# A mixture-of-experts stage whose short last groups become single tiles of their own

## The chip, the cores and the metric

The kernel runs on one core of a Trainium2 chip. The metric is the device time of one execution in microseconds, taken as the median of several executions. The engines are named as in the profile: PE is TensorE (PEld its weight loads), DVE is VectorE, ACT is ScalarE, POOL is GpSimd, SP is SyncE.

## The reference

The reference is a small network layer over 4 x 1024 tokens of 256 channels in fp32: a recurrent block, then an attention block, then a mixture of four experts, with normalizations and residual sums around them. The change touches the mixture alone. What it computes, cut to that part:

```python
logits = xf @ gate_w.T                      # xf: (4096, 256), E = 4 experts, K = 2
probs = softmax(logits)
topv, topi = top_k(probs, K)
topv = topv / (topv.sum(-1, keepdims=True) + 1e-08)
wts = zeros((N, E)).at[arange(N)[:, None], topi].add(topv)
o0 = gelu(xf @ e0_up.T) @ e0_down.T                                   # HID = 512
o1 = silu(xf @ e1_w1.T) * (xf @ e1_w2.T) @ e1_down.T
o2 = gelu(gelu(gelu(xf @ e2_l1.T) @ e2_l2.T) @ e2_l3.T) @ e2_l4.T
o3 = gelu(gelu(xf @ e3_down.T) @ e3_up.T) @ e3_out.T
moe = sum over e of wts[:, e:e+1] * o_e       # first 64 channels set to zero
x = x + layernorm(x_in_block + moe)
```

Every token uses exactly two of the four experts, so there are six kinds of tokens, one for each pair of experts.

## The kernel before

Nearly all of the program is written as streams of operations (generators that yield an `Op` with engine, cost, priority and the events that it needs). `Plan.run` interleaves the streams by the earliest start that its cost model gives, and the order that comes out is the fixed order of the instructions on each engine. An engine runs its instructions strictly in that order, so an instruction that waits holds up all that stand behind it on its engine.

The expert stage works on kinds. `experts_input` gives every token a place in the list of its kind with matrix products, and writes the lists to `ids` (for each of 6 kinds 32 columns of 128 token numbers; unused places point at a row of zeros). The counts of the six kinds go to `counts`, and each engine loads them into registers once (L1614).

A kind is worked on in groups of N = 256 tokens, that is two tiles of 128 (`NT2 = 2`). For each group:

- `fetch` gathers the rows of the tokens from DRAM with one indirect DMA for each tile (L1414, on POOL, tiles `rwfirst`, `rwsecond`, `rwnext`);
- `turn` scales the rows on DVE (L1428), transposes them on PE (L1435) into a PSUM bank, and copies them to SBUF on ACT (L1441);
- `group` multiplies with the weights of the two experts: `products` on PE (L1456 for the hidden layers, 256 tokens wide; L1475 for the down products, one for each tile), `activations` on ACT (L1516 gelu, L1523 tanh) with two DVE products for the gated expert 1 (L1526, L1532), `outputs` on DVE (L1543), and `last`, which normalizes (DVE L1556, L1557, L1568, L1571; POOL L1562, L1563) and scatters the rows to the output (L1574, on POOL).

The kinds follow each other in the order 3, 0, 1, 2, 4, 5. The first group of each kind is always run; each further group stands inside an `If` on the count of the kind (L1620), nested in the group before. Where the `If` is not taken, every engine jumps behind all the further groups of the kind. At the place that it jumps to it brings its semaphores to the values that they would have had; POOL does so with `INC_SWDGE_SEM` for those of its DMAs. On PE a hint for the branch is given a group ahead (L1595).

What is prepared in a group for later ones stands in the list `then`: the rows of the second next group of the kind are fetched, the next group is turned, and in the first group of a kind the rows of the first two groups of the second next kind are fetched and the first group of the next kind is turned. The first group of kind 3 (`EARLY`) is run while the gates of the last tokens are still being computed, and has a list of its own.

PSUM banks are split by whether a group is a kind's first (`"first"`: two banks for hidden layers, one for outputs) or a later one (`"next"`: three and one), with one bank for all transposes (`tbanks`).

## Time and profile before

| | |
|---|---|
| median of 3 executions | 1489.87 us |
| lowest and highest | 1489.75 and 1490.87 us |
| time of the profiled execution | 1487.5 us |
| its span, first to last instruction | 1485.7 us |
| mean granted PE clock | 0.943 |
| PE, DVE, ACT, POOL busy | 1327.7, 873.2, 723.9, 467.5 us |
| last instruction of PE that is busy ends | about 1464 us |

The span is counted from the first instruction. In the lists in order of time the columns are start, duration, engine, line, operation, the tiles written and read, and in brackets the idle time of the engine ahead of the instruction and what ended it. In the list of stages the columns are the stretch, its length, the busy time of PE, PEld, DVE, ACT and POOL with the number of instructions, the granted PE clock, the busy share of the DMA engines and the rate in GB/s. A name with a `q` behind the engine (`POOLq`) is that of the engine's sequencer; its branches, semaphore instructions and drains are not counted as busy. For a line of the kernel the profile gives the durations in ns as least, median and greatest, and the times of the first and last.

### The profile page before, as it was taken

Reading aid. Unit: us, or ns where it says so; the run is one execution under the profiler, and the core shown is the slowest. Engines: PE = TensorE matmul, PEld = TensorE weight load, DVE = VectorE, ACT = ScalarE, POOL = GpSimd, SP = SyncE. Lnnn points to the kernel's source line nnn. Section 1 sums busy time; section 2 is a strip of 40 time slices with the busy share of each in tenths; the row PEclk is TensorE's granted clock in tenths of the full one; section 3 lists DMA queues with packets and bytes.
Section 4 is the critical chain, followed back from the end, with each engine's and each line's share of the span. In section 5 each row is a group of like instructions: output and inputs, shape, how many; then the busy total and the mean of one; then the engine's idle time right before and its main releaser. Section 6 shows DMA issues by size and latency. Waiting matters only on the chain. (4 is left out here: it accounts for less than half of the span.)

```text
span 1485.7 us, 43429 instructions
## 1 busy us (share of the span) xinstructions
PE 1327.7 (89%) x17800; PEld 1055.8 (71%) x17800; DVE 873.2 (59%) x2419; ACT 723.9 (49%) x2176; POOL 467.5 (31%) x1465
## 2 busy tenths in 40 slices
PE   4568668989999999899999999999999999999994
PEld 2225536656777777777787678878788889888883
DVE  5566668678687588668768776775414312113331
ACT  2345545756756766776654455556422222223220
POOL 2433534535444444344211100101143321214321
PEclk8778878999999999999999999999999999999997
DMA  3010010001010000000001000222031110102200
GB/s 126 29 43 1 15 44 2 16 16 30 3 30 17 2 31 17 3 31 17 3 3 32 17 3 3 56 84 75 16 108 58 51 59 26 40 23 76 56 28 23
DMA packets 35207, 48.73 MB, mean 33 GB/s; under 512 B 7574, under 2 KB 27286, under 8 KB 34966
## 3 DMA queue, kind: packets, MB, share of 16 engines
q1 hardware_dynamic: 28134, 24.94, 5.5%
q0 software_dynamic: 6560, 20.09, 4.7%
q8 instruction: 147, 2.41, 0.7%
q14 instruction: 94, 0.77, 0.2%
q10 hardware_dynamic: 272, 0.52, 0.1%
HBM read 32.34 MB, written 13.73 MB: 31 GB/s over the span
## 5 line engine op out<-in xcount | busy, mean ns | idle before, releaser
L937 DVE TENSOR_REDUCE nm<-bank 128x1 f32<-128x512 f32 (+4 forms) x656 | 373.3, 618 | 144.2 <-PE bank L898 103.4
L979 ACT ACTIVATE ex<-bank 128x512 f32<-128x512 f32 (+1 forms) x592 | 325.7, 581 | 159.3 <-PE bank L855 102.2
L855 PE MATMUL bank<-keys,q 32*128 32x128 f32 x4608 | 346.8, 290 | 14.4 <-ACT ex L979 5.0
L554 POOL TENSOR_TENSOR s<-keys 128x8 f32<-128x8 f32 x1023 | 224.8, 220 | 374.5 <-ACT keys L557 364.1
L855 PE MATMUL bank<-q,keys 32*128 32x128 f32 x4608 | 333.2, 292 | 3.7 <-ACT ex L979 2.4
L557 ACT ACTIVATE keys<-s 128x8 f32<-128x8 f32 x1023 | 218.3, 213 | 206.8 <-POOL s L554 204.5
L855 PEld LDWEIGHTS bank<-q,keys 32*128 32x128 f32 x4608 | 267.9, 190 | 67.9 <-issue 29.6
L855 PEld LDWEIGHTS bank<-keys,q 32*128 32x128 f32 x4608 | 285.0, 190 | 39.0 <-DVE nm L937 13.9
L999 POOL TENSOR_SCALAR_AFFINE_SELECT ex<-ex 128x256 f32<-128x256 f32 (+1 forms) x240 | 103.2, 431 | 290.2 <-ACT ex L979 286.2
L1016 PE MATMUL av<-ex,values 128*17 128x128 f32 x4608 | 162.5, 282 | 2.6 <-DVE avT L1035 2.0
L1456 PE MATMUL bank<-values,keys 128*128 128x256 f32 x632 | 149.5, 383 | 4.7 <-PEq L1620 3.3
L1016 PEld LDWEIGHTS av<-ex,values 128*17 128x17 f32 x4608 | 117.3, 100 | 27.9 <-issue 10.0
L1456 PEld LDWEIGHTS bank<-values,keys 128*128 128x128 f32 x632 | 118.5, 191 | 21.5 <-issue 4.7
L1516 ACT ACTIVATE keys<-bank 128x256 f32<-128x256 f32 x136 | 52.2, 384 | 156.1 <-PE bank L1456 156.0
L1456 PE MATMUL bank<-keys 128*128 128x256 f32 x384 | 84.8, 379 | 0.0
L764 PE MATMUL bank<-ident,pad 128*128 128x128 f32 x384 | 61.5, 293 | 25.8 <-DVE pad L715 23.0
L1456 PEld LDWEIGHTS bank<-keys 128*128 128x128 f32 x384 | 73.0, 190 | 9.9
L505 PE MATMUL bank<-big,wsg 128*128 128x512 f32 x128 | 71.8, 710 | 9.0 <-ACT big L443 5.9
L764 PEld LDWEIGHTS bank<-ident,pad 128*128 128x128 f32 x384 | 45.4, 149 | 36.1 <-ACT keys L557 19.1
L1543 DVE SCALAR_TENSOR_TENSOR rwnext<-av,rwnext 128x192 f32<-128x192 f32 x28 | 10.4, 413 | 101.6 <-PE av L1475 101.6
L1516 ACT ACTIVATE hid<-bank 128x256 f32<-128x256 f32 x66 | 25.4, 384 | 89.5 <-PE bank L1456 89.5
L1475 PE MATMUL av<-keys 128*128 128x192 f32 x384 | 66.4, 326 | 0.0
(232 smaller groups left out, 1687.6 us busy)
## 6 DMA issues: line engine op xcount, KB each, us to landing
row_d<-xn SPq DMA_DIRECT2D x16, 512.0 KB
xn<-in_x SPq DMA_DIRECT2D x8, 512.0 KB
xc<-in_x SPq DMA_DIRECT2D x7, 512.0 KB
keys<-in_e_l SPq DMA_DIRECT2D x2, 1024.0 KB
keys<-in_e_w SPq DMA_DIRECT2D x2, 512.0 KB
keys<-in_e_down SPq DMA_DIRECT2D x2, 384.0 KB
rwnext<-row_d,ids POOLq DMA_INDIRECT x36, 3.8
xc<-in_x SPq DMA_DIRECT2D x4, 128.0 KB
```

What stands on the lines that cost most here:

```text
L505: nc.tensor.matmul(pb, lhsT=wsg[:, cc, half * C + dc * P : half * C + (dc + 1) * P], rhs=lnT[:, cc, :], start=(cc == 0), stop=(cc == NCC - 1),
L554: nc.gpsimd.tensor_tensor(s, st[:, :, t], prev, ALU.add)
L557: nc.scalar.activation(st[:, :, t], s, AF.Tanh)
L764: nc.tensor.transpose(banks.tiles[pb][:, hc * P : (hc + 1) * P], flat[:, side, hc * P : (hc + 1) * P], ident,)
L855: nc.tensor.matmul(banks.tiles[pbs[j]][:, m * P : (m + 1) * P], lhsT=k if kind == "sT" else q, rhs=q if kind == "sT" else k, start=(m == 0 ...
L937: nc.vector.tensor_reduce(by_slot[:, half, h0:h1, 2 * p + j], banks.tiles[pb][:, m0 * P : m1 * P].rearrange("p (h w) -> p h w", h=h1 - h0) ...
L979: nc.scalar.activation(exs.tiles[ex[1]][:, j, : step.w], banks.tiles[pb][:, : step.w], AF.Exp)
L999: nc.gpsimd.affine_select(out=d, in_=d, pattern=pattern, compare_op=ALU.is_ge, fill=0.0, base=0, channel_multiplier=-1,)
L1016: nc.tensor.matmul(av[32 * j : 32 * j + HD + 1, hc, :], lhsT=v_all[:, b, kb, 4 * hc + j, :], rhs=exs.tiles[ex[j // 2][1]][:, j % 2, m * P ...
L1456: nc.tensor.matmul(hb[0].tiles[hb[1]], lhsT=w[:, j, m * P : (m + 1) * P], rhs=src[:, j, :], start=(j == 0), stop=(j == nk - 1),)
L1475: nc.tensor.matmul(ob[0].tiles[ob[1]][:, t, :], lhsT=src[:, j, t * P : (t + 1) * P], rhs=w[:, j, :], start=(j == 0), stop=(j == nk - 1),)
L1516: nc.scalar.activation(to, src, AF.Gelu)
```

## The change

A kind's last group is handled apart if no more than 128 tokens are left for it. The `If` of a further group now asks for more than 128 tokens beyond the groups before, so such a rest no longer runs as a group of 256. In its place there are six tails, one for each kind, each a group of one tile of 128 tokens behind all kinds and under a branch of its own. A kind that has no such rest, or only its first group, jumps over its tail.

For this the list of a tail is computed on DVE behind `ids`: a second six counts (0 where there is no tail), and for each kind the one column of the list that belongs to the tail (`tails`). Each kind's tail has buffers of its own for its rows and its transposed rows (`rwtail`, `xtail`). The rows of a kind's tail are gathered and turned in the first group of the next kind, those of the last kind in its own first group, whether there is a tail or not. The operations of `turn` and `group` get the width of one tile for a tail; the costs that the planner is told stay those of a group of 256.

```diff
-        counts=const.tile([1, KINDS], I32, name="counts"),
+        counts=const.tile([1, 2 * KINDS], I32, name="counts"),
+        tails=const.tile([P, KINDS], U32, name="tails"),
...
+                yield Op("DVE", 2.0, 80.0, [ev("ids")])
+                n = stat.tile([P, 3, KINDS], I32, tag="whole", name="n")
+                nc.vector.tensor_copy(n[:, 0], base)
+                nc.vector.tensor_scalar(n[:, 1], n[:, 0], 2 * P - 1, None, ALU.bitwise_and)
+                nc.vector.tensor_scalar(n[:, 2], n[:, 0], 8, None, ALU.logical_shift_right)
...
+                nc.vector.tensor_copy(route["counts"][:, KINDS:], nf[0:1, 0])
...
+                for c in range(KINDS):
+                    yield Op("DVE", 0.5, 80.0)
+                    nc.vector.scalar_tensor_tensor(
+                        ids, ramp, nf[:, 1, c : c + 1], listed, ALU.is_equal, ALU.mult,
+                        accum_out=over[:, c : c + 1],
+                    )
+                yield Op("DVE", 0.4, 80.0)
+                nc.vector.tensor_scalar(over, over, -1.0, float(TOKENS), ALU.mult, ALU.add)
+                nc.vector.tensor_copy(route["tails"], over)
+                done("tails")
...
+    rows["tail"] = slots(KINDS, [P, 1, ROW], "rwtail").tiles
+    x_tail = slots(KINDS, [P, NCC, P], "xtail").tiles
...
-        for t in range(NT2):
-            yield Op("POOL", 1.25, at, [ev("ids")], lag=3.0)
+        for t in range(tiles_of(g)):
+            yield Op("POOL", 1.25, at, [ev("tails" if g == TAIL else "ids")], lag=3.0)
...
         if g == 0:
             then += [fetch(kind(n + 2), 0), fetch(kind(n + 2), 1)]
-            if n + 1 < KINDS:
+            for before in [order[n - 1]] if n else []:
+                then += [fetch(before, TAIL), turn(before, TAIL)]
+            if n + 1 == KINDS:
+                then += [fetch(c, TAIL), turn(c, TAIL)]
+            else:
                 then.append(turn(kind(n + 1), 0))
...
             with tc.If(
-                n_of[c] > (g + 1) * N, preferred_fallthrough_block=True, label=label
+                n_of[c] > (g + 1) * N + P, preferred_fallthrough_block=True, label=label
             ):
                 groups(c, g + 1)
...
     for c in order:
         groups(c, 0)
+    for n, c in enumerate(order):
+        hint(f"tail{n}", KINDS + c, 0)
+        with tc.If(n_of[KINDS + c] > 0, preferred_fallthrough_block=True, label=f"tail{n}"):
+            group(c, TAIL, [])
```

More of the change, by code (lines that the diff above doesn't have):

```diff
@@ L1233, in experts_input @@
                 yield Op("DVE", 1.1, prio)
-                nc.vector.tensor_scalar(listed, listed, -1.0, float(TOKENS), ALU.mult, ALU.add)
-                nc.vector.tensor_copy(route["ids"], listed)
+                ids = rows.tiles[0][:, :LISTS]
+                nc.vector.tensor_scalar(ids, listed, -1.0, float(TOKENS), ALU.mult, ALU.add)
+                nc.vector.tensor_copy(route["ids"], ids)
                 nc.vector.tensor_tensor(base, base, first, ALU.subtract)
-                nc.vector.tensor_copy(route["counts"], base[0:1])
+                nc.vector.tensor_copy(route["counts"][:, :KINDS], base[0:1])
@@ L1238, in experts_input @@
                 done("ids")
+                yield Op("DVE", 2.0, 80.0, [ev("ids")])
[3 more added lines that the diff above has]
+                nc.vector.tensor_scalar(n[:, 2], n[:, 0], 8, None, ALU.logical_shift_right)
+                nf = stat.tile([P, 3, KINDS], F32, tag="nf", name="nf", bufs=1)
+                nc.vector.tensor_copy(nf[:, :2], n[:, 1:3])
@@ new lines, in experts_input @@
+                over = nf[:, 2]
+                nc.vector.tensor_scalar(over, nf[:, 0], float(P), None, ALU.is_le)
+                nc.vector.tensor_tensor(nf[:, 0], nf[:, 0], over, ALU.mult)
+                nc.vector.tensor_scalar(over, nf[:, 1], 0.5, None, ALU.is_gt)
+                nc.vector.tensor_tensor(nf[:, 0], nf[:, 0], over, ALU.mult)
+                nc.vector.tensor_copy(route["counts"][:, KINDS:], nf[0:1, 0])
+                nc.vector.tensor_scalar(over, nf[:, 0], 0.5, None, ALU.is_lt)
@@ new lines, in experts_input @@
+                nc.vector.scalar_tensor_tensor(
+                    nf[:, 1], over, float(LISTS), nf[:, 1], ALU.mult, ALU.add
+                )
+                nc.vector.tensor_scalar(first, first, 1.0 / P, None, ALU.mult)
+                nc.vector.scalar_tensor_tensor(
+                    nf[:, 1], nf[:, 1], 2.0, first, ALU.mult, ALU.add
+                )
+                for c in range(KINDS):
+                    yield Op("DVE", 0.5, 80.0)
+                    nc.vector.scalar_tensor_tensor(
+                        ids, ramp, nf[:, 1, c : c + 1], listed, ALU.is_equal, ALU.mult,
+                        accum_out=over[:, c : c + 1],
+                    )
@@ L1389, in kind, with xT_of, tiles_of @@
         return order[n] if n < KINDS else None
+    TAIL = "tail"
+    x_tail = slots(KINDS, [P, NCC, P], "xtail").tiles
     def of(c, g):
+        if g == TAIL:
+            return "next", turn_of[c]
         return ("first", turn_of[c] % 2) if g == 0 else ("next", g % 2)
+    def xT_of(c, g):
+        what, k = of(c, g)
+        return x_tail[k] if g == TAIL else xTs[what][k]
+    def tiles_of(g):
+        return 1 if g == TAIL else NT2
     def rows_of(c, g):
@@ L1397, in rows_of @@
         n = turn_of[c]
+        if g == TAIL:
+            return rows["tail"][n]
         what, k = ("first", n) if g == 0 else ("second", n) if g == 1 else ("next", g)
@@ L1403, in ids_of @@
             return route["early"][:, t : t + 1]
+        if g == TAIL:
+            return route["tails"][:, c : c + 1]
         at = (c * TOKENS + g * N) // P + t
@@ L1407, in fetch @@
     def fetch(c, g, at=0.0):
-        if c is None or g * N >= TOKENS:
+        if c is None or g != TAIL and g * N >= TOKENS:
             return
         rw = rows_of(c, g)
-        for t in range(NT2):
-            yield Op("POOL", 1.25, at, [ev("ids")], lag=3.0)
+        for t in range(tiles_of(g)):
+            yield Op("POOL", 1.25, at, [ev("tails" if g == TAIL else "ids")], lag=3.0)
             nc.gpsimd.indirect_dma_start(
@@ L1422, in turn @@
         what, k = of(c, g)
-        rw, x = rows_of(c, g), xs[what][0]
-        for t in range(NT2):
+        nt = tiles_of(g)
+        rw, x = rows_of(c, g), xs["first" if g == TAIL else what][0]
+        for t in range(nt):
             got = yield Op("DVE", 0.36, 3.0, [ev("rows", c, g, t)], [] if t else [tbanks["any"]])
@@ L1431, in turn @@
             done("xs", c, g, t)
-        yield Op("PE", 0.6, 5.0, [ev("xs", c, g, t) for t in range(NT2)], lag=0.2)
+        yield Op("PE", 0.6, 5.0, [ev("xs", c, g, t) for t in range(nt)], lag=0.2)
         for cc in range(NCC):
-            for t in range(NT2):
+            for t in range(nt):
                 nc.tensor.transpose(
@@ L1440, in turn @@
         yield Op("ACT", 0.62, 0.5, [ev("xT0", c, g)])
-        nc.scalar.copy(xTs[what][k], tb[0].tiles[tb[1]])
+        nc.scalar.copy(xT_of(c, g), tb[0].tiles[tb[1]][:, :, : nt * P])
         give(tb)
@@ L1445, in group @@
     def group(c, g, then):
-        what, k = of(c, g)
+        what, _ = of(c, g)
         me = (c, g)
-        xT, rw = xTs[what][k], rows_of(c, g)
+        nt = tiles_of(g)
+        w_ = nt * P
+        xT, rw = xT_of(c, g), rows_of(c, g)
         hid_, t_s, hb_, ob_ = hids[what], ts[what], hbanks[what], obanks[what]
@@ L1456, in product @@
                 nc.tensor.matmul(
-                    hb[0].tiles[hb[1]], lhsT=w[:, j, m * P : (m + 1) * P], rhs=src[:, j, :],
+                    hb[0].tiles[hb[1]][:, :w_], lhsT=w[:, j, m * P : (m + 1) * P],
+                    rhs=src[:, j, :w_],
                     start=(j == 0), stop=(j == nk - 1),
@@ L1467, in products @@
                 if how == "down":
-                    for t in range(NT2):
+                    for t in range(nt):
                         got = yield Op(
@@ L1509, in activations @@
                         yield Op("ACT", 0.0, prio, [ev("h", me, e, n, m, name)])
-                    src = hb_.tiles[made[key][1]]
+                    src = hb_.tiles[made[key][1]][:, :w_]
                     hid = made["hid", e, n]
-                    to = hid_.tiles[hid[1]][:, m, :]
+                    to = hid_.tiles[hid[1]][:, m, :w_]
                     if how == "up":
@@ L1521, in activations @@
                     t_, = yield Op("ACT", 0.4, prio, [ev("h", me, e, n, m, name)], [t_s])
-                    t = t_s.tiles[t_[1]]
+                    t = t_s.tiles[t_[1]][:, :w_]
                     nc.scalar.activation(t, src, AF.Tanh, scale=0.5)
@@ L1531, in activations @@
                     yield Op("DVE", 0.45, prio, [ev("h", me, e, n, m, "v1")])
-                    nc.vector.tensor_tensor(to, hb_.tiles[made[key][1]], t, ALU.mult)
+                    nc.vector.tensor_tensor(to, hb_.tiles[made[key][1]][:, :w_], t, ALU.mult)
                     give(made[key], t_)
@@ L1539, in outputs @@
             ob = made["o", e]
-            for t in range(NT2):
+            for t in range(nt):
                 yield Op("DVE", 0.42, prio, [ev("o", me, e)])
@@ L1552, in last @@
             mv = stat.tile([P, NT2, 2], F32, tag="mv5", name="mv5")
-            for t in range(NT2):
+            for t in range(nt):
                 yield Op("DVE", 0.6, 3.0, [ev("y", me, e, t) for e in pairs[c]])
@@ L1561, in last @@
             r = stat.tile([P, NT2], F32, tag="r5", name="r5")
-            nc.gpsimd.tensor_scalar(z, mv[:, :, 1], LN_EPS, None, ALU.add)
-            nc.gpsimd.tensor_tensor(r, z, mhalf[:, :NT2], ALU.pow)
+            z, r = z[:, :nt], r[:, :nt]
+            nc.gpsimd.tensor_scalar(z, mv[:, :nt, 1], LN_EPS, None, ALU.add)
+            nc.gpsimd.tensor_tensor(r, z, mhalf[:, :nt], ALU.pow)
             done("r", me)
-            for t in range(NT2):
+            for t in range(nt):
                 yield Op("DVE", 0.85, 3.0, [ev("r", me)])
@@ L1593, in groups @@
         if more and n_of:
-            tc.mark_branch_hint_location(
-                label, n_of[c] > (g + 1) * N, engines=[mybir.EngineType.PE]
-            )
+            hint(label, c, (g + 1) * N + P)
         then = [fetch(c, g + 2)]
@@ L1620, in groups, with hint @@
             with tc.If(
-                n_of[c] > (g + 1) * N, preferred_fallthrough_block=True, label=label
+                n_of[c] > (g + 1) * N + P, preferred_fallthrough_block=True, label=label
             ):
                 groups(c, g + 1)
+    def hint(label, c, at):
+        tc.mark_branch_hint_location(label, n_of[c] > at, engines=[mybir.EngineType.PE])
     n_of = []
```

## The prediction

> **What bounds the kernel now.** First the page's span and busy row, then its slices, then the stages of the expert part, then the lists of single engines in time order.

> ```profile
> span 1485.7 us, 43429 instructions
> PE 1327.7 (89%) x17800; PEld 1055.8 (71%) x17800; DVE 873.2 (59%) x2419; ACT 723.9 (49%) x2176; POOL 467.5 (31%) x1465
> PE   4568668989999999899999999999999999999994
> ```

> ```profile
> 1174.00:1334.00 160.00, 158.90 (x796) 143.40 (x796) 28.81 (x86) 40.98 (x103) 33.67 (x40) 1.00 0.12 37
> 1464.00:1486.00 22.00, 0.01 (x1) 0.00 (x0) 3.34 (x10) 0.00 (x0) 2.99 (x4) 0.56 0.04 13
> ```

> Inside a kind TensorE is the bound (158.9 of 160 us, clock 1.00). But after its last matmul there are 22 us in which it does nothing, and VectorE and GpSimd only 3 us each. So the expert stage has two prices: per group that of TensorE, and at the end that of a serial chain, most of it in sequencers, which the busy columns do not show.

> TensorE in kind 2 (experts 0 and 3), one line per piece:

> ```profile
> 1349.21 0.60 PE L1435 MATMUL bank<-ident,values 128*128 128x128 f32 x4
> 1350.54 2.86 PE L1456 MATMUL bank<-values,keys 128*128 128x256 f32 x12 [0.73 <-ACT values L1441]
> ...
> 1364.92 2.75 PE L1456 MATMUL bank<-values,keys 128*128 128x256 f32 x12
> ...
> 1379.19 2.75 PE L1456 MATMUL bank<-values,keys 128*128 128x256 f32 x12
> ```

> A whole group takes 1379.19 - 1364.92 = 14.27 us. GpSimd in the first group of the same kind, which TensorE began at 1334.84:

> ```profile
> 1347.37 1.01 POOL L1414 DMA_INDIRECT rwnext<-row_d,ids  x1 [4.62 <-issue]
> ...
> 1353.72 0.95 POOL L1414 DMA_INDIRECT rwsecond<-row_d,ids  x1 [0.30 <-issue]
> DMA to landing us min/median/max: 3.3/3.8/4.4
> ```

> Its gathers begin 12.5 us after TensorE's start, since GpSimd still finishes the group before and then does the branch. Six of them run 1.25 us apart, and the last lands at 1358. TensorE is through with this group at 1350.5. Today that is harmless: they fetch for later groups. Last, the branch L1620, six exits from kinds on GpSimd, and the drain at the end:

> ```profile
> L1620 POOLq INC_SWDGE_SEM  x1: 620/620/620, 1134.7 to 1134.7; - x1
> L1620 POOLq INC_SWDGE_SEM  x1: 910/910/910, 1183.7 to 1183.7; - x1
> L1620 POOLq INC_SWDGE_SEM  x1: 1462/1462/1462, 1344.8 to 1344.8; - x1
> L1620 POOLq INC_SWDGE_SEM  x1: 1867/1867/1867, 1404.1 to 1404.1; - x1
> L1620 POOLq INC_SWDGE_SEM  x1: 2027/2027/2027, 1445.7 to 1445.7; - x1
> L1620 POOLq INC_SWDGE_SEM  x1: 2107/2107/2107, 1474.8 to 1474.8; - x1
> ```

> ```profile
> L1683 POOLq DRAIN  x3: 46/103/7998, 1476.9 to 1485.5; - x3
> ```

> Each not-taken branch costs GpSimd one INC_SWDGE_SEM, and it grows. GpSimd's DMAs issued before the six are 20, 36, 64, 84, 92 and 96: all six fit 0.19 us + 0.020 us for each. How much work is jumped over does not order them (the third skips fewer groups than the first and takes twice as long).

> **What it removes.** The reference run on its inputs gives kinds 0 to 5 744, 1496, 836, 456, 320 and 244 tokens: rests of 232, 216, 68, 200, 64 and 244 after whole groups of 256. Only kinds 2 and 4 have a rest of 1 to 128; four of the six tails are jumped over. Gone are kind 2's fourth group, 14.27 us, and kind 4's second, from 1417.14 to 1435.04, 17.90 us. Sum -32.2 us.

> **What it adds ahead of the tails.**
> - List work on VectorE: 13 small instructions at 0.2 us and six over 192 columns at 0.4 us, 5 us behind 1076.6. VectorE waits there until 1080.1 for a gather, and the rows it then scales are needed by TensorE at 1089. Cost 0. Were that cover gone, 5 us.
> - Twelve counts to load instead of six: TENSOR_LOAD took 0.93 to 1.05 us for six, so 1 us more. TensorE's load at 1091.8 lies under matmuls queued to 1094.2. Cost 0.
> - In each first group of the kinds behind the first: a gather, a VectorE scaling (0.35), two transposes (0.22 of TensorE) and an ACT copy, unconditionally. This is the part that I think decides. The gather is issued and used in the same group, and in GpSimd's built order it stands behind all six other gathers. In VectorE's order the scaling stands before the group's last accumulations or normalization, and in TensorE's the transposes stand at the group's end (in kind 4's, before its last products). All are in order, so nobody passes a late row.
>  Kind 0: seventh gather at 1142.78 + 1.25 = 1144.03, landing 3.7 later (the sixth took 3.6), scaling and hop 0.4, transposes 0.22: next group at 1148.4 instead of 1141.58, +6.8.
>  Kind 1: the row is there (TensorE's group lasts to 1202), but the next group's transposes now wait for the tail's copy and for VectorE work put in front: 1204.5 instead of 1202.2, +2.3.
>  Kind 2: 1354.98 + 4.4 (the sixth took 4.4) + 0.4 + 0.2 = 1360.0 instead of 1350.54, +9.45.
>  Kind 4: two gathers before it, 1409.6 + 4.3 = 1413.9. VectorE then still owes TensorE's two PSUM banks their products; I follow the last two quarters of the hidden layer through and get the end at 1419.5 instead of 1417.14, +2.4.
>  Kind 5: rows land before they are needed; two pairs of transposes, +0.44.
>  Sum +21.4 us. Nothing of it is hidden: TensorE has no slack there.

> TensorE thus ends kind 5 at 1463.98 - 32.2 + 21.4 = 1453.2, 10.8 us early.

> **What it adds behind.** GpSimd's exit from kind 5 ended at 1476.89 (1474.76 + 2.11 + hop), now 1466.1. Then come three tails to jump over (kinds 3, 0, 1). Each has branch and waits (0.4) and an INC_SWDGE_SEM. 96 - 8 + 6 = 94 DMAs went before, so 0.19 + 0.020 x 94 = 2.07. No row shows an INC for a single skipped DMA: bounds 0 and 2.1; I take 2.07, since the six rows follow the count issued. So 3 x 2.45 = 7.35, and GpSimd is free at 1473.4.

> Matters for the jump itself: VectorE's not-taken branches left it idle 2.7 to 3.0 us, e.g.

> ```profile
> 1401.03 0.42 DVE L1526 SCALAR_TENSOR_TENSOR tfirst<-tfirst,bank 128x256 f32<-128x256 f32 x1 [2.73 <-DVEq L1620]
> ```

> while the short branch right behind such an exit cost 0.2. [...] By the long rows alone it would be 3 x 2.8 and GpSimd 8 us later. [...]

> The first executed tail (kind 2, 6.96 us of TensorE at half the records and half the pitch of 0.216 us) is done with its statistics before 1473, even with slow jumps on TensorE or VectorE. So GpSimd's z and r come last: r after 1.06 us, VectorE's normalization 0.9, and VectorE is at kind 4's tail at 1475.4. Its gated hidden layer stalled behind that normalization: with three PSUM banks TensorE could do only the first quarter. From there, with VectorE pieces of 0.3 to 0.4 (0.42 at 256 columns) and TensorE pieces of 0.44, the remaining quarters and the down product take 3.9 us; accumulation, statistics, r, normalization up to the scatter another 3.6 (3.87 before for two tiles): scatter at 1482.9. After it: 1.06 issue, 0.4 to the exit of the last tail, INC 2.15, drain 8.0, 0.8 of barriers = 12.4. Span 1495.3. In one line: -32.2 + 21.4 + 7.35 + (21.9 - 8.8 from the last common exit to the end) = +9.6 us.

> The profiled execution took 1487.5 us with a span of 1485.7; the median of the three runs is 1489.87, 2.4 above. Adding 9.6 to the median: 1499.5 us.

> **Rivals.** What a measurement of this kernel can tell from no change is about 0.2%, 3 us.
> (a) Faster: the tail rows arrive in time, because GpSimd reaches them sooner than in the trace. Price: the 20 us of waiting less. Against it stand the gathers at +11.5 and +12.5 us in kinds 0 and 2. It decides once the waits sum to under 8.8 us instead of 21.4; wholly without waits the time is near 1479. Chance 0.13.
> (b) The INC costs by the work skipped, and is near 0 for one DMA: four times 2.1 less, 1491. For it: nothing but that it would be natural. Chance 0.12 (together with half-sized waits: no change).
> (c) The jumps are long ones: 1507. Chance 0.17.
> (d) The forecast: 0.58.
> That the change doesn't do what it says is possible only in that four of six tails are empty, which is in the sum.

> Range 1490 to 1508: it reaches (b) and (c) and leaves out most of (a). Faster 0.13, same 0.12, slower 0.75.

> **What would show it.** Right: in kinds 0 and 2 TensorE idle 6 to 10 us before the transposes of the tail, ended by VectorE, which was waiting for the gather into rwtail; INC_SWDGE_SEM ten times, the last four near 2.1 us; the tails' TensorE work waiting on VectorE and that on GpSimd's r; over 40 us from TensorE's last whole group to the end. Wrong: transposes without idle time before them, INCs of some 0.1 us, or tails in which TensorE is dense.

## The result, and the profile after

The changed kernel took 1511.87 us (median of four runs, 1506.0 to 1516.41) against 1490.37 us before (median of four, 1489.75 to 1493.4). The ratio is 1.0133, interval 1.0115 to 1.0152: slower by about 21 us. The forecast was 1499.5 us, +9.6, with a range up to 1508: the measured time lies above it, and the loss is more than twice the one forecast. The waits that were forecast are there; the half clock behind them, and the order of the last work on TensorE, were not in the forecast. The profiled execution took 1508.23 us, with a span of 1506.4 us.

The span, the busy row and the slices of the changed kernel's page, as they were shown of before:

```profile
span 1506.4 us, 43457 instructions
PE 1320.3 (88%) x17772; PEld 1049.8 (70%) x17772; DVE 875.3 (58%) x2436; ACT 722.4 (48%) x2180; POOL 464.8 (31%) x1465
PE   5568569899999999899998999999998999997875
```

TensorE has 7 us less to do in a span that is 21 us longer: what was added is time in which it stands. In the list of TensorE's waits in the expert part (the columns are engine, tile and line, what it waited for, the sum, the times, and the longest), nearly all of it has two causes.

```profile
PE bank L1490 <- DVE values L1483: 21.8, 4, 9.6
PE bank L1513 <- DVEq L1694: 7.8, 1, 7.8
PE bank L1513 <- DVE tnext L1584: 4.1, 1, 4.1
PE bank L1513 <- PEq L1680: 3.4, 4, 1.8
```

The first line is the scaled rows of the tails, late in four first groups. The next two lie behind the whole groups, at the two tails that are executed. Before, all of TensorE's listed waits in the expert part came to 7.1 us, and the longest was 1.9.

The first cause in the lists in order of time. GpSimd in kind 0's first group, then TensorE in that group and in kind 2's:

```profile
1141.95 0.95 POOL L1468 DMA_INDIRECT rwsecond<-row_d,ids  x1 [0.30 <-issue]
1143.20 0.95 POOL L1468 DMA_INDIRECT rwtail<-row_d,tails  x1 [0.30 <-issue]
```

```profile
1138.06 2.76 PE L1533 MATMUL bank<-keys,hid 128*128 128x192 f32 x16
1147.67 0.66 PE L1490 MATMUL bank<-ident,values 128*128 128x128 f32 x2 [6.85 <-DVE values L1483]
...
1371.64 0.66 PE L1490 MATMUL bank<-ident,values 128*128 128x128 f32 x2 [9.64 <-DVE values L1483]
```

The tail's gather is the last of seven on GpSimd. TensorE waits 6.85 us in kind 0 and 9.64 us in kind 2, where 6.8 and 9.45 were forecast. What the forecast did not have comes right behind. Stages of the changed kernel (columns as for the stages of before; the granted TensorE clock is the third number from the end):

```profile
1139.49:1142.91 3.42, 1.34 (x9) 1.04 (x7) 0.00 (x0) 0.00 (x0) 2.79 (x3) 1.00 0.75 203
1142.91:1146.32 3.41, 0.00 (x0) 0.00 (x0) 0.00 (x0) 0.00 (x0) 0.95 (x1) 0.50 0.60 204
1146.32:1149.74 3.42, 2.06 (x6) 1.75 (x7) 2.01 (x7) 0.37 (x1) 0.22 (x1) 0.50 0.02 10
1149.74:1153.15 3.41, 3.41 (x9) 2.69 (x9) 2.26 (x6) 0.77 (x2) 1.79 (x2) 0.50 0.00 0
1153.15:1156.56 3.41, 3.41 (x19) 3.18 (x19) 0.42 (x1) 1.15 (x3) 1.25 (x2) 1.00 0.11 38
```

The clock falls to 0.50 during the wait and is still there when the row has come: in the fourth stretch TensorE is busy all the time and does 9 matmuls, in the fifth, of the same length, 19. The clock is back 5.5 us after the end of the wait. Summing what the distance of consecutive starts exceeds the one at full clock, TensorE lost 2.7 us in kind 0 in this way, 1.6 in kind 2, 1.4 in kind 4, and 1.8 and 2.6 in the two executed tails. The kernel before had one such stretch, 1.8 us in kind 4, behind two stalls of 0.53 and 1.89 us:

```profile
1398.34:1401.75 3.41, 1.37 (x5) 0.92 (x6) 0.72 (x3) 0.48 (x2) 1.06 (x2) 1.00 0.08 25
1401.75:1405.16 3.41, 3.41 (x9) 2.66 (x9) 0.23 (x1) 0.38 (x1) 0.45 (x1) 0.50 0.02 5
1405.16:1408.57 3.41, 3.41 (x21) 3.31 (x21) 0.43 (x1) 0.38 (x1) 1.21 (x2) 1.00 0.00 0
```

It could have been read there, and was passed over. The rows are cut at borders of the stretches of 3.41 us in which the two profiles record the granted clock: from 1055 us on, where the experts' work lies, it changes at such borders alone, and it goes with how much of the stretch before TensorE was busy. In these two profiles it fell from 1.00 to 0.50 ten times, each time behind a stretch that was busy up to 0.46 of its length (here 1.34 of 3.42 us, and 1.37 of 3.41), and stayed at 1.00 behind all that were busy 0.49 or more. It came back eight times, behind stretches busy 0.83 or more, and not behind those busy 0.60 or less (here not behind 2.06 of 3.42 us). So it took no long wait in the kernel before: the stalls of 0.53 and 1.89 us were enough.

The end. TensorE in the two executed tails (kind 2's from 1466.87, kind 4's from 1475.78):

```profile
1458.73 0.38 PE L1490 MATMUL bank<-ident,values 128*128 128x128 f32 x2
1466.87 2.90 PE L1513 MATMUL bank<-xtail,keys 128*128 128x128 f32 x12 [7.76 <-DVEq L1694]
...
1477.12 1.07 PE L1513 MATMUL bank<-keys,values 128*128 128x128 f32 x8
1482.28 2.08 PE L1513 MATMUL bank<-keys,values 128*128 128x128 f32 x8 [4.09 <-DVE tnext L1584]
1484.15 1.06 PE L1513 MATMUL bank<-xtail,keys 128*128 128x128 f32 x4
1485.00 2.77 PE L1533 MATMUL av<-keys 128*128 128x192 f32 x8
1487.56 2.95 PE L1513 MATMUL bank<-xtail,keys 128*128 128x128 f32 x24
1490.35 1.47 PE L1533 MATMUL av<-keys 128*128 128x192 f32 x8
```

Before the first tail it waits 7.76 us for VectorE's sequencer. Behind the second wait there are 9.5 us of matmuls still to do, the first 20 of them at half clock. Then the branches' semaphore increments on GpSimd (least, median and greatest ns), VectorE's normalization of the first tail, and the branches over the tails on the sequencers:

```profile
L1680 POOLq INC_SWDGE_SEM  x6: 620/1677/2067, 1133.9 to 1470.8; - x6
L1694 POOLq INC_SWDGE_SEM  x4: 2041/2052/2080, 1473.2 to 1495.5; - x4
```

```profile
1476.97 0.18 DVE L1615 BATCH_NORM_AGGREGATE mv<-st 128x2 f32<-128x6 f32 x1
1481.15 0.41 DVE L1627 TENSOR_SCALAR rwtail<-rwtail,mv,r 128x256 f32<-128x256 f32 x1 [4.00 <-POOL r L1622]
```

```profile
L1694 PEldq COMPARE_BRANCH  x8: 82/216/2340, 1459.5 to 1491.6; - x8
L1694 ACTq COMPARE_BRANCH  x8: 38/42/50, 1461.6 to 1490.3; - x8
L1694 DVEq COMPARE_BRANCH  x8: 47/53/63, 1466.2 to 1495.1; - x8
```

A skipped tail costs GpSimd 2.05 us for one skipped DMA, as forecast, and the first tail's normalization waits 4.0 us for GpSimd's r. TensorE's sequencer (in the rows PEldq) spends up to 2.3 us in one branch over a tail.

### The profile page after: what moved, and what is told of

It is laid out like the page before. It is cut to its first block, busy times and chain, and to the rows that moved or that the text cites. A ratio compares the mean times of both kernels' runs of the same rounds, so it can differ in the third digit from the quotient of the medians.

```text
span 1506.4 us, 43457 instructions
## 1 busy us (share of the span) xinstructions
PE 1320.3 (88%) x17772; PEld 1049.8 (70%) x17772; DVE 875.3 (58%) x2436; ACT 722.4 (48%) x2180; POOL 464.8 (31%) x1465
## 5 line engine op out<-in xcount | busy, mean ns | idle before, releaser
L1513 PE MATMUL bank<-values,keys 128*128 128x256 f32 x568 | 138.6, 392 | 4.8 <-PEq L1680 3.4
L1574 ACT ACTIVATE keys<-bank 128x256 f32<-128x256 f32 (+1 forms) x136 | 50.5, 372 | 160.0 <-PE bank L1513 158.2
L1513 PEld LDWEIGHTS bank<-values,keys 128*128 128x128 f32 x568 | 109.4, 197 | 21.2 <-issue 4.5
L765 PEld LDWEIGHTS bank<-ident,pad 128*128 128x128 f32 x384 | 44.4, 146 | 35.9 <-ACT keys L558 19.7
L1621 POOL TENSOR_SCALAR z<-mv 128x2 f32<-128x2 f32 (+1 forms) x18 | 4.1, 226 | 205.1 <-DVE mv L1615 193.7
L683 PE MATMUL bank<-wqk,big 128*128 128x512 f32 x128 | 64.5, 632 | 2.6 <-ACT big L444 2.6
```

The source lines that it names most:

```text
L683: nc.tensor.matmul(pqk, lhsT=hT[:, cc, b * P : (b + 1) * P], rhs=wqk[:, cc, :], start=(cc == 0), stop=(cc == NCC - 1),)
L765: nc.tensor.transpose(banks.tiles[pb][:, hc * P : (hc + 1) * P], flat[:, side, hc * P : (hc + 1) * P], ident,)
L1513: nc.tensor.matmul(hb[0].tiles[hb[1]][:, :w_], lhsT=w[:, j, m * P : (m + 1) * P], rhs=src[:, j, :w_], start=(j == 0), stop=(j == nk - 1),)
L1574: nc.scalar.activation(to, src, AF.Gelu)
```

## The experiments

Each ratio is to executions of the kernel before on the same chip; a version was executed 4 to 20 times. The part of the program before kind 0 takes up to 7 us more or less than in the profile of before, from one execution to the next (12 us more in the last version). So beside the ratio of the times each row gives the stretch from TensorE's first product of kind 0 to the end of the span, read in the one profiled execution: 360.8 us before, 382.3 after. The forecast of +9.6 is 370.4 on this scale. It is one execution for each version: four whose whole groups are the same (the changed kernel and experiments 3, 6 and 7) agree within 0.4 us up to the last whole group, but whether a short stall brings half clock differs from one profile to another, and that is up to 1.8 us. Ratio and stretch agree within some 3 us in all rows, so the part before kind 0 has no cost above that.

| version | ratio to before, interval | kind 0 to the end, us |
|---|---|---|
| changed kernel | 1.0133, 1.0115 to 1.0152 | 382.3 |
| turn in the tail | 0.9976, 0.9965 to 0.9987 | 357.0 |
| two tails in the program | 1.0061, 1.0040 to 1.0083 | 370.3 |
| no tail taken | 1.0297, 1.0266 to 1.0327 | 408.2 |
| tail's gather first | 1.0005, 0.9991 to 1.0019 | 358.3 |
| TensorE kept busy in two waits | 1.0105, 1.0062 to 1.0148 | 378.6 |
| gather first, tails in between | 1.0032, 1.0018 to 1.0046 | 363.9 |
| gather in the own kind | 1.0000, 0.9983 to 1.0018 | 361.9 |
| the same, tails in between | 1.0036, 1.0020 to 1.0052 | 363.2 |
| r on VectorE in the tails | 1.0148, 1.0118 to 1.0178 | 382.5 |
| turn in the tail, dummies in all tails | 1.0031, 1.0011 to 1.0051 | 363.5 |
| gated expert last in kind 4's tail | 1.0123, 1.0094 to 1.0153 | 377.2 |
| turn in the tail, dummies in kind 4's | 0.9987, 0.9977 to 0.9996 | 356.2 |

**1. The wait for the rows: turned where they are used.**

```diff
-                then += [fetch(before, TAIL), turn(before, TAIL)]
+                then += [fetch(before, TAIL)]
...
-            group(c, TAIL, [])
+            group(c, TAIL, [turn(c, TAIL)])
```

> The gathers of the tails stay where they are, but the scaling, transposes and copy of a tail are done in the tail itself. Theory W (the loss is TensorE waiting for tail rows in the kinds' first groups, and running at half clock after each long wait): the idle time before the tails' transposes (6.9, 1.6, 9.6 and 3.7 us) and the half-clock stretches behind it (2.7, 1.6, 1.4 us) go, about 29 us; the two executed tails get 1 to 2 us longer each. Span about 1480 against 1506.4 for the changed kernel, time about 1484, ratio to before about 0.996. Rival E (the loss is the serial end: six branches, GpSimd's exits, the tails' own chains): TensorE's last whole group may end earlier, but the time stays above 1500.

Measured: 0.9976, 25.3 us shorter than the changed kernel from kind 0 to the end, where 29 less 2 to 4 were expected. The waits of 6.9, 9.6 and 3.7 us in the first groups are gone, and so are the half-clock stretches behind them. This is the only kind of version here that is faster than before.

**2. The wait for the rows: the gather ahead of the others.** TensorE's, VectorE's and ScalarE's instructions keep their order; only GpSimd's gathers change places.

```diff
-                then += [fetch(before, TAIL), turn(before, TAIL)]
+                ahead = 1.25 * (6 if n < 4 else 2)
+                then += [fetch(before, TAIL, -1.0, 3.0 + ahead), turn(before, TAIL)]
```

> In kinds 0, 1, 2 and 4 the tail's gather is put ahead of the group's other gathers on GpSimd; the planner is told a lag longer by as much, so that the order on TensorE, VectorE and ScalarE stays exactly that of the changed kernel. Theory W: the rows land 7.5 us (kind 4: 2.5 us) earlier, the idle times before the tails' transposes in kinds 0, 2 and 4 go, with the half-clock stretches behind them: 26 us less, span about 1481, time about 1485. Kind 1's 2.2 us stay. If the waits come from anything else than the place of the gather (VectorE's order, the copies on ScalarE), nothing changes: about 1510.

Measured: 1.0005, 24.0 us shorter than the changed kernel. Since nothing but the place of five gathers on one queue differs, late rows cost 24 us in all: the waits themselves, and what followed from them. Kind 1's group, in which the rows never were late, kept its waits of 1.6 and 0.7 us, and kind 2's kept 2.1 us for VectorE's scaling. In the time itself this version does not part from the kernel before.

**3. Skipped tails left out of the program.**

```diff
     for n, c in enumerate(order):
+        if c not in (2, 4):
+            continue
```

> Of the six tails only those of kinds 2 and 4 are left in the program; the four that are empty with these inputs have no branch. Gathers and turns stay. Theory W: four INC_SWDGE_SEM of 2.05 us go, three of them ahead of the first executed tail, but its statistics are ready only 3 us before GpSimd is, so the gain is about 4 us there and 2 us at the end: time about 1506. Rival E: nearly all of the 21 us of loss goes, about 1491.

Measured: 12.0 us shorter than the changed kernel, twice the 6 expected: the two waits of the tails are shorter as well, which the expectation did not have. TensorE in this version:

```profile
1468.52 2.20 PE L1513 MATMUL bank<-xtail,keys 128*128 128x128 f32 x12 [2.53 <-ACTq L1680]
...
1480.90 1.16 PE L1513 MATMUL bank<-keys,values 128*128 128x128 f32 x8 [1.18 <-DVE tnext L1584]
```

The first tail starts 2.5 us behind the whole groups, not 7.8 us, and it no longer waits for VectorE, which still normalizes kind 5's last rows at that time. And behind the second wait, 1.2 us instead of 4.1, the granted clock is 1.00 (in 1480.9 to 1484.0): the eight products there take 1.16 us instead of 2.08.

**4. All tails skipped.** The condition for a whole group is the old one, and the second six counts are zeroed, so that six tails are jumped over and none is executed.

```diff
-                n_of[c] > (g + 1) * N + P, preferred_fallthrough_block=True, label=label
+                n_of[c] > (g + 1) * N, preferred_fallthrough_block=True, label=label
```

> The split alone is undone: a further group asks for any tokens beyond the groups before, as in the kernel before, and the second six counts are zero, so that six tails are jumped over; gathers, turns, lists and branches of the tails all stay. This gives the bare overhead. Theory W: the waits and half-clock stretches stay (28 to 30 us) and six GpSimd exits of 2.4 us come to the end (14 us): about 1533. Rival E: only the end is longer, about 1504.

Measured: 1.0297, and a profiled span of 1529.9 us. GpSimd's sequencer:

```profile
L1696 POOLq INC_SWDGE_SEM  x6: 2201/2201/2218, 1505.8 to 1518.4; - x6
```

Six increments begin 2.5 us apart after the last kind's own, with nothing executed between them: a serial tail of 15 us that no other engine covers. They are 0.15 us longer than in the changed kernel, since the whole groups that run again issue more DMAs.

**5. The half clock: TensorE kept busy while it waits.** Nothing is sooner here; TensorE merely transposes the identity into the bank that the tail's transposes will overwrite.

```diff
+        for _ in range(({1: 56, 3: 80}.get(turn_of[c] + 1, 0) if g == TAIL else 0)):
+            nc.tensor.transpose(tb[0].tiles[tb[1]][:, 0, 0:P], ident, ident)
```

> The changed kernel with dummy transposes of the identity on TensorE (56 in kind 0's first group, 80 in kind 2's) put directly ahead of the tail's own transposes, so that TensorE works while it waits for the tail's rows; nothing else is changed, and the rows come no sooner. If the half clock after those waits comes from the idle time itself (6.9 us in kind 0, 9.6 in kind 2), the matmuls behind them run at full rate at once and the 2.7 us and 1.6 us lost there vanish: the stretch from kind 0 to the end is some 4 us shorter than the 382.3 us of the changed kernel, near 378. If the slow matmuls have another reason (late operands, a throttle of the chip), they stay slow and the stretch stays at 382 or grows by what the dummies overrun.

Measured: 378.6 us, 378 expected. In its stages, the dummies and then the first products behind them, in kind 0 and kind 2:

```profile
1144.20:1150.70 6.50, 6.50 (x60) 6.48 (x59) 0.00 (x0) 0.00 (x0) 3.14 (x4) 1.00 0.68 202
1152.60:1157.00 4.40, 4.40 (x21) 3.88 (x22) 2.96 (x11) 1.86 (x5) 1.73 (x3) 1.00 0.00 0
1373.80:1379.00 5.20, 5.20 (x26) 4.57 (x25) 1.85 (x5) 2.29 (x6) 2.05 (x2) 1.00 0.07 25
```

The clock is 1.00 where it was 0.50, with the operands as late as before. So in these two waits it was the idle time that halved the clock, not the lateness of the operands. The ratio alone (1.0105) does not part from that of the changed kernel, as the intervals overlap; the stages and the stretch do.

**6. Where the last matmuls go: the gated expert behind the other in kind 4's tail.**

```diff
+        if g == TAIL and eb == 1:
+            plan.run([*then, products(ea, 1.0), activations(ea, 1.0), outputs(ea, 1.0)])
+            plan.run([products(eb, 2.0), activations(eb, 2.0), outputs(eb, 2.0), last()])
+            return
```

> The changed kernel with the order inside the executed tail of kind 4 changed alone: all matmuls of the one expert (b3, u3, d3) are put ahead of the gated expert's (u1, v1, d1), instead of the two in turns. In the changed kernel TensorE stood behind a gated product's bank from 1478.0 to 1482.3, with 9.8 us of matmuls still to come once VectorE arrived. If that fixed order is why the last 9.8 us came where 3.9 were forecast, the ungated expert's work moves in front of VectorE's arrival: some 4 us less, 378 us from kind 0 to the end. If what follows VectorE's arrival is bound by the gates on VectorE one after the other, under 1 us.

Measured: 377.2 us, 378 expected. TensorE in kind 4's tail:

```profile
1484.42 1.10 PE L1513 MATMUL bank<-xtail,keys 128*128 128x128 f32 x8
1485.48 2.27 PE L1513 MATMUL bank<-keys,values 128*128 128x128 f32 x16
1487.59 1.47 PE L1533 MATMUL av<-keys 128*128 128x192 f32 x8
1488.90 3.86 PE L1513 MATMUL bank<-xtail,keys 128*128 128x128 f32 x32
1492.59 1.47 PE L1533 MATMUL av<-keys 128*128 128x192 f32 x8
```

The other expert's 32 records are done when VectorE gets through with the first tail's normalization, at 1489.0. TensorE has no wait left in the second tail, and from 1489.0 to the scatter it is 8.5 us instead of 13.3. Up to kind 4's tail the engines' instructions are those of the changed kernel. In it eight of the gated expert's matmuls move behind the other's work, and with them one tanh on ScalarE and one output on VectorE change places, so the order was what the forecast had wrong there. The ratio again does not part the two kernels by itself.

**7. GpSimd's r taken out of the chain.** In the tails, VectorE computes the inverse root by itself.

```diff
+                by.tensor_scalar(z, mv[:, :nt, 1], LN_EPS, None, ALU.add)
+                by.tensor_scalar(
+                    r.bitcast(I32), z.bitcast(I32), 1, None, ALU.logical_shift_right
+                )
...
+                for _ in range(3):
+                    by.tensor_tensor(q, r, r, ALU.mult)
```

> The changed kernel; in the tails alone the inverse root of the variance is taken on VectorE (eleven instructions on one column: a first guess from the number's bits and three Newton steps) instead of GpSimd's two. In the changed kernel the first tail's mean and variance were there at 1477.2, but GpSimd reached z only at 1480.2, behind its exits of the skipped tails, and VectorE came to the second tail at 1481.9. If the exits delay the end through z and r, VectorE comes to the second tail at about 1479.6 on the same scale and the stretch from kind 0 to the end falls by some 2 us, from 382.3 to 380. If TensorE's own lateness in the tails sets the end, no gain (382 to 383).

Measured: 382.5, no gain. From the start of the first tail to VectorE's arrival at the second it took 14.4 us instead of 15.1, although 0.9 us more went to half clock in between. From the variance to the normalization it was 4.0 us in the first tail of the changed kernel and 1.1 us in its second, where GpSimd is free: the exits held the first tail back by 2.9 us. Here it is 2.4 us in both, twelve VectorE instructions 0.19 us apart. The first tail gains 1.6 us and the second loses 1.3, so the exits are in the chain but this is no remedy.

**8. The tails between the kinds.** In the version with the gather first, each tail's branch stands behind the next kind's whole groups.

```diff
     for n, c in enumerate(order):
         groups(c, 0)
+        if n:
+            tail(n - 1)
+    tail(KINDS - 1)
```

> The version with the tail's gather ahead of the other gathers, and each kind's tail branch put behind the next kind's whole groups instead of behind all of them, the last kind's tail at the end. Theory: GpSimd's exits of skipped tails (2.4 us each) then lie beside whole groups and leave the serial end, and kind 2's executed tail runs amid whole groups: from kind 0 to the end about 354 us (358.3 with the gather first alone, 360.8 before), 4 us better than that version. Rival: the tails' branches amid the whole groups break up the overlap at a kind's border (each kind has to load its operands again, and engines wait for each other's exits at every tail), and what the end gains is paid there: 360 or more.

Measured: 363.9, the rival. The waits of TensorE in the expert part, and a kind's border:

```profile
PE bank L1513 <- PEq L1694: 8.9, 3, 4.6
PE bank L1513 <- DVEq L1681: 7.3, 1, 7.3
...
PE bank L1513 <- ACTq L1681: 2.8, 1, 2.8
```

```profile
1341.50 5.48 PE L1513 MATMUL bank<-values,keys 128*128 128x256 f32 x12 [4.63 <-PEq L1694]
```

The exits leave GpSimd's end, but TensorE's own branches over tails now stop it at three borders of kinds, 8.9 us in all (in the version with the gather first, its branches at the borders stopped it 4.6 us), and it still waits 7.3 and 2.8 us ahead of the two executed tails. Half clock follows there too (the 12 products take 5.5 us; they took 2.8 in the middle of a kind).

**9. Gathers in the tail's own kind,** so that they are a kind's length early; tails at the end, and tails between the kinds.

```diff
+            then += [fetch(c, TAIL)]
...
-                then += [fetch(before, TAIL), turn(before, TAIL)]
+                then += [turn(before, TAIL)]
```

> The changed kernel with each tail's rows gathered in its own kind's first group and turned in the next kind's first group, a kind's whole length later; tails stay at the end. Theory: the rows are always there, so that no first group waits for them (kind 1's 2.2 us too) and no half clock follows: about 25 us less than the changed kernel, 357 us from kind 0 to the end, some 3 us under before. Rival: the gather takes the place of another one on GpSimd's queue, and then the first group waits for that one (ids of the next group) instead: 365 or more.

> As the run before (gathers in the own kind's first group), with the tail branches put behind the next kind's whole groups. If the skipped tails' exits on GpSimd are what keeps the end long, 4 to 5 us less than with the tails at the end: about 352 us from kind 0 to the end. If the broken overlap at the borders costs as much, no gain or a loss.

Measured: 361.9 and 363.2, both short of the forecast (357 and 352). In the first the rows are in time, but three stalls of 1.3 to 1.9 us, behind VectorE's scaling in kinds 1 and 2 and behind its gated product in kind 4, were each followed by a half-clock stretch that cost 1.7 to 1.8 us (in kind 1 TensorE was busy 1.39 of the 3.41 us before it; kind 4's was there before the change too). In the second the borders cost the same as in experiment 8 (TensorE waits 8.9 us for its own branches at L1694). Both miss the gain for these reasons as far as the waits show; no run took them apart.

**10. The best version, kept busy.** The version of experiment 1, with dummy transposes ahead of the tails' transposes: in all tails (72 for kind 2, 30 for kind 4, 40 for the others), then 32 in kind 4's alone.

```diff
+        for _ in range(32 if (c, g) == (4, TAIL) else 0):
+            nc.tensor.transpose(tb[0].tiles[tb[1]][:, 0, 0:P], ident, ident)
```

> The version with the turn in the tail (357.0 us from kind 0 to the end, 0.9976 of before), with dummy transposes of the identity on TensorE ahead of the transposes in each tail (72 for kind 2, 30 for kind 4, 40 for the others). There TensorE stood idle 9.6 and 3.8 us at the two executed tails and then ran at half clock for a loss of 2.7 and 2.2 us. If idle time is what halves the clock, most of these 4.9 us go: about 353 us, 0.995 of before. Rival: the tails are bound by VectorE and ScalarE, not by TensorE's rate, and the gain is under 2 us; or the dummies overrun the wait and cost what they gain.

> The version with the turn in the tail (0.9976 of before, 357.0 us from kind 0 to the end) with 32 dummy transposes of the identity in the tail of kind 4 alone. In the run with dummies in all tails the 30 of this tail ran inside TensorE's wait of 3.8 us and the matmuls behind them took 10.2 us instead of 12.4, while the 72 of the first executed tail began only after the wait and cost 10.4 us. Without those, some 2.2 us less than the version with the turn in the tail: 355 us, 0.996 of before. If the second tail is bound by VectorE and ScalarE after all, no gain (357).

With dummies in all tails 363.5 us, the rival. TensorE at the first executed tail, and its branches over tails:

```profile
1433.90 2.76 PE L1535 MATMUL bank<-keys,hid 128*128 128x192 f32 x16
1447.71 10.61 PE L1489 MATMUL bank<-ident 128*128 128x128 f32 x72 [11.04 <-PEq L1696]
```

```profile
L1696 PEldq COMPARE_BRANCH  x8: 82/335/3729, 1437.0 to 1479.8; - x8
```

What TensorE waited for there was not a row but its own sequencer: three branches over skipped tails, 2.7 to 3.7 us each. The dummies stand behind them, so they came after the wait instead of in it, and cost 10.4 us. In the second tail they did what was expected. With dummies in that tail alone, the second tail's first and second products of the plain version and of this one:

```profile
1460.45 2.93 PE L1513 MATMUL bank<-xtail,keys 128*128 128x128 f32 x12 [0.46 <-ACT xtail L1496]
1463.17 2.71 PE L1513 MATMUL bank<-keys,values 128*128 128x128 f32 x16
```

```profile
1469.29 1.60 PE L1515 MATMUL bank<-xtail,keys 128*128 128x128 f32 x12 [0.46 <-ACT xtail L1498]
1470.73 2.01 PE L1515 MATMUL bank<-keys,values 128*128 128x128 f32 x16
```

The same matmuls take 1.6 and 2.0 us instead of 2.9 and 2.7, and from the tail's transposes to its last product it is 10.1 us instead of 12.3. Of these 2.2 us the stretch shows 0.8 (356.2 against 357.0): in this execution kind 4's first group lost 1.8 us to half clock, as in the kernel before, which it did not in the other. The ratio, 0.9987 (0.9977 to 0.9996, on another chip), is under before but does not part from 0.9976. So turning the rows in the tail is faster than the kernel before by 0.24% (0.13 to 0.35), and than the changed kernel by some 1.5%; that the dummies add to it is shown in the tail, not in the time.

## Why the prediction was right in direction and less than half in size

On the scale from kind 0 to the end the forecast was 370.4 and the measurement 382.3: 11.9 us were missing.

- **Waits in the first groups, "+6.8, +2.3, +9.45, +2.4, +0.44":** measured waits of 6.85, 9.64 and 3.73 us in kinds 0, 2 and 4, and next groups that came 2.1 us later in kind 1 and 0.45 in kind 5. In kind 2 some luck is in it: the tail's gather was issued 1.1 us sooner after TensorE's start than forecast, and took 5.0 us to land instead of 4.4. In kind 4 the row came when it was forecast (19.9 us after TensorE's start of the kind, 19.7 forecast). The wait is 1.3 us longer than the 2.4 forecast because TensorE was there sooner: it had no half clock in this group before the wait, as it had had in the kernel before. Experiments 1 and 2 show the cause: take away the lateness of the rows and 24 to 25 us go.
- **"TensorE ends kind 5 at 1453.2":** it ended at 1459.1, with kind 0 begun 0.8 us earlier: 6.7 us late. This is the first step that failed. Each wait was counted by its length alone, as if TensorE went on at its old rate. Behind the waits in kinds 0, 2 and 4 it lost 5.7 us at half clock, and 1.1 us more at the border of kinds 1 and 2 (idle 1.75 us instead of 0.62). Experiment 5 shows for kinds 0 and 2 that the idle time is the cause of the half clock (1.00 with the dummies, 0.50 without); why that border grew, no run shows.
- **List work and loads of counts, "Cost 0":** not contradicted. The part before kind 0 was 0.8 us shorter than before, but it varies by more than that, so a small cost would not show.
- **GpSimd's exits, "3 x 2.45", and 94 DMAs:** right. Each took 2.05 us and they came 2.4 us apart. Rival (b), a price by the work skipped, falls: the exits that skip one DMA took 2.04 to 2.08 us, the one before them, over a kind's further groups, 2.07.
- **"VectorE is at kind 4's tail at 1475.4", 22.2 us behind TensorE's last whole group:** 22.8 us measured, with GpSimd's r last, as forecast.
- **The jump over a tail, taken as short (inside the 0.4 for branch and waits in each 2.45):** that was the author's estimate, from the branch of 0.2 us behind an exit from a kind. No run shows it as the price of such a jump; in its place the changed kernel showed 0.04 to 0.06 us in the branch on VectorE, ScalarE and GpSimd, and on GpSimd 0.3 us from one increment's end to the next one's start. So rival (c), whose 1507 is nearest to the measured time, is not what happened. On TensorE the three branches took 0.9, 0.2 and 2.3 us. It did not decide: TensorE was through them at 1464.3 and then waited for VectorE, which got to the tails only at 1466.1, behind its normalization and a long exit from kind 5. TensorE began the first executed tail about 0.15 us after VectorE's exit from the second skipped one (1466.70). In experiments 2, 5 and 6 and the first version of experiment 9, too, its wait there, 7.5 to 7.8 us, ended with VectorE's sequencer; with dummies in all tails (experiment 10) it was 11.0 us and ended with its own. That TensorE's start would have such a gate at all was not in the forecast.
- **"The remaining quarters and the down product take 3.9 us":** 9.9 us measured (1481.94 to 1491.82). This is the second step that failed. Gated products, other expert's products and down products are in one fixed order on TensorE; the forecast took the other expert's work as done during the wait, but with the three banks full it stood behind the blocked product. Then 2.6 us of half clock came on top, after the wait of 4.1 us. Experiment 6 moves that work ahead and gets 4.8 us of the 13.3 to the scatter back.
- **"12.4 after the scatter":** 11.1. From VectorE's arrival to the end, with 7.5 us forecast to the scatter and 13.3 measured, this stretch is 4.5 us late; with the 0.6 of the arrival, 5.1.

In sum 6.7 and 5.1, the 11.9 us that were missing within 0.1. The corrected sum: -32.2 for the groups removed, 21.4 + 6.7 = 28.1 for the waits and what followed from them, and 20.5 + 5.1 = 25.6 at the end, +21.5 us. Rival (a) describes experiments 1 and 2: with the rows in time the change gains, but only 3.8 and 2.5 us on this scale, and in the times 0.24% and nothing that shows, not the 11 us forecast.

On the half clock, the kernel before lost 1.8 us behind the stretch in kind 4 that was busy 1.37 of 3.41 us. At that price, an estimate from this one stretch, the forecast would have had some 1.8 us more behind each of its waits of 6.8 and 9.45 us in kinds 0 and 2. Kind 2's 1.6 us agrees; kind 0's 2.7 is more: behind the stretch in which its wait ended, with 2.06 us of work in 3.42, the clock was still 0.50.

## What to carry to other kernels

Price a new wait on TensorE with its length and with the stretch at half clock behind it (1.4 to 2.7 us in the changed kernel), and count short stalls together (0.53 and 1.89 us were followed by 1.8 us lost in the kernel before): look at the granted clock directly behind the stalls that the trace already has. A gather that is issued and used in one group belongs at the head of its queue, or its use belongs where the data is surely there; here that alone was worth 24 us, more than the whole loss. A branch over work that is skipped is itself work on every engine: for each skipped tail of the changed kernel 2.04 to 2.08 us in GpSimd's semaphore increment, 0.2 to 2.3 us in TensorE's branch, 0.04 to 0.06 us in those of VectorE and ScalarE. Work split off into small pieces at the end pays that for every piece that is skipped: six of them made a serial tail of 15 us in experiment 4, and leaving out four was worth 12.0 us in experiment 3.
